# Two attention and expert layers on one core: loads reordered, first batch's layer norm in groups, clearing stores moved

## The chip, the cores and the metric

The kernel runs on one core of a Trainium2 chip. A core has five engines with their own instruction queues: TensorE (PE, matrix products), VectorE (DVE), ScalarE (ACT), GpSimd (POOL) and SyncE (SP, which here only issues transfers). Sixteen DMA engines move data between the chip's memory and the core's on-chip memory; SP, ACT and POOL can issue to them. The metric is the device time of one execution in microseconds (us). Before the change it is 3061.97 us, the median of 3 runs (3060.4 to 3063.5).

## The reference

Four sequences of 512 rows of 256 numbers (`x`) pass four layers, each added to `x`: a cross attention, a routed expert layer, a second cross attention, a second expert layer. The change touches the first alone:

```python
xn = _layernorm(x, gamma_media, beta_media)      # x here: the context, 4 x 1601 x 256
ln = _layernorm(latents, gamma_lat, beta_lat)    # latents: the normalised x, 4 x 512 x 256
q = ln @ Wq + bq
kv_input = jnp.concatenate([xn, ln], axis=1)
kv = kv_input @ Wkv + bkv
k, v = jnp.split(kv, 2, axis=-1)
...
sim = jnp.einsum('bhid,bhjd->bhij', q, k)        # 8 heads of 128
attn = jax.nn.softmax(sim, axis=-1)
out = jnp.einsum('bhij,bhjd->bhid', attn, v)
...
return out @ Wo + bo
```

The latents are normalised twice: once by the caller, once here with their own weights. Keys and values run over 512 + 1601 = 2113 positions. All numbers are float32.

## The kernel before

The kernel is written in a tile language: the source gives operations on tiles, and a scheduler decides the place of each operation in its engine's queue, from the dependences between tiles, from buffers coming free and from its own estimate of times. An engine works through its queue in that order, so an operation that waits holds up all that stand behind it on the same engine. The order in the source is a priority and no promise.

**Set-up (lines 66 to 332).** Constants and masks; among them `iota_i`, `lane_i` and `number_i` (lines 154, 306, 310), whole numbers that GpSimd writes and VectorE casts to float. `slot_x` and `rows_x` are tables in the chip's memory for the two expert layers. They are cleared once: `clear_slots` (line 147) with 8 stores of 512 KB issued by GpSimd, `clear_rows` (line 334) with 32 stores of 530 KB and one of 265 KB issued by SyncE, all out of a tile `empty`. `slot_x` is first written when batch 0 is routed, `rows_x` not before the last layer.

**First attention (lines 476 to 842).** Loads go out on SyncE in the order x of batch 0, seven small vectors (layer norm weights `gbm`, `gbl`, biases `bqk`), `bo`, the context of batch 0 as one transfer (12 tiles of 128 rows) and its tail of 65 rows, `wq`, `wkv`, `wo`, x of the other batches. `keys_input` (line 528) prepares a batch: `moments` (row statistics, bn_stats and bn_aggr, of 13 context tiles), `scale` (one square root on ScalarE for all tiles, then small VectorE operations, `ln_scale`, line 101), `latents` and `latents_again` (the two norms of x), `apply` (normalising the context, on VectorE), and `group` (line 551), which transposes four tiles on TensorE and evacuates them with the weights applied into `kvin`: channels 0 to 127 on VectorE, 128 to 255 on ScalarE. `kvin` holds position (k x 17 + c) x 32 + i at block c, quarter k, element i: each 128-wide block has 32 positions of each quarter of the sequence. The output bias `bo` gets the values' bias through `wo`: 8 rounds of a VectorE copy into `values_bias` and a product on TensorE (lines 742 to 749); `latents_again` adds `bo` to x on GpSimd.

`queries_keys(h)` (line 605) projects queries and keys of a head in six pieces, five of them keys, of 512 columns of `kvin` in the order of memory (the last of 128). `values` (line 648) projects the values for two heads in pieces of two blocks.

The loop at line 769 runs over n = batch x head x row tile, 128 steps. In step n: `scores` (5 products into the one buffer `ps_s`, then the maximum on VectorE, line 687), `turn` of the step before (a 32 x 32 transpose on VectorE, line 708), `softmax` (exponential on ScalarE, line 693), `exchange` (16 transfers of 68 KB between partition groups, 12 issued by SyncE and 4 by ScalarE, line 700), every second step `project`, and `weigh` (17 products for two row tiles, spread over two steps, line 716). `later[n]` holds pieces of other work for step n, such as the next head's keys. Before the loop, batch 0 is prepared in the order of the source (lines 751 to 756), then `empty` is set and both tables are cleared.

Transfers share eight completion semaphores for SyncE and ScalarE and eight for GpSimd. A transfer waits at issue until the one that holds its semaphore, in general the eighth before it, has landed.

Of the kernel before, what the change touches and what calls it, by code (L numbers as in the profile page):

```python
# [8 lines left out]
F32 = mybir.dt.float32  # L9
I32 = mybir.dt.int32  # L10
AF = mybir.ActivationFunctionType
ALU = mybir.AluOpType
# [4 lines left out]
P = 128  # L17
B, S, D = 4, 512, 256
M = 1601
NT = S // P  # L20
# [19 lines left out]
E, FF = 8, 1024  # L40
FC = FF // P
CAP = 2 * B * S // E
SLOTS = E * CAP
CT = CAP // P
NOWHERE = 65536.0
# [3 lines left out]
T = B * S  # L49
G = 256  # L50
GR = G // P
NG = (2 * T + E * (G - 1)) // G
ROWS = E * T
PAY = D + 1 + E
# [5 lines left out]
def rows_of(i, n, tail):  # L60
    return tail if i == n - 1 else P


@with_exitstack
def xattn_ffn_twice(ctx: ExitStack, tc: tile.TileContext, a: dict, out: bass.AP):
    nc = tc.nc

    const = ctx.enter_context(tc.tile_pool(name="const", bufs=1))
    dram = ctx.enter_context(tc.tile_pool(name="dram", bufs=1, space=DRAM))

    ident = const.tile([P, P], F32, name="ident")
    make_identity(nc, ident)

    flip = [0]

# [25 lines left out]
    def ln_scale(pool, mv, n):  # L101
        ve = pool.tile([P, n], F32, tag=f"ve{n}", name="ve")
        nc.vector.tensor_scalar(ve, mv[:, :, 1], EPS, None, ALU.add)
        rs = pool.tile([P, n], F32, tag=f"rs{n}", name="rs")
        nc.scalar.activation(rs, ve, AF.Sqrt)
        nc.vector.reciprocal(rs, rs)

        t = pool.tile([P, n], F32, tag=f"nt{n}", name="t")
        nc.vector.tensor_tensor(t, rs, rs, ALU.mult)
        nc.vector.tensor_tensor(t, t, ve, ALU.mult)  # L110
        nc.vector.tensor_scalar(t, t, -0.5, 1.5, ALU.mult, ALU.add)
        nc.vector.tensor_tensor(rs, rs, t, ALU.mult)
        return mv, rs
# [30 lines left out]
    slot_y = dram.tile([SLOTS, D], F32, name="slot_y")  # L144
    rows_x = dram.tile([ROWS + G, PAY], F32, name="rows_x")

    def clear_slots(zeros):
        for i in range(SLOTS // (4 * P)):
            nc.gpsimd.dma_start(
                slot_x[i * 4 * P : (i + 1) * 4 * P, :].rearrange("(p r) d -> p r d", p=P), zeros  # L150
            )


    iota_i = const.tile([P, NT, E], I32, name="iota_i")
    nc.gpsimd.iota(iota_i, pattern=[[0, NT], [1, E]], base=0, channel_multiplier=0)
    iota = const.tile([P, NT, E], F32, name="iota")
    nc.vector.tensor_copy(iota, iota_i)
# [4 lines left out]
    for r in (32, 96):  # L162
# [6 lines left out]
        fill=0.0,  # L169
# [133 lines left out]
                )  # L303


    lane_i = const.tile([P, 1], I32, name="lane_i")
    nc.gpsimd.iota(lane_i, pattern=[[0, 1]], base=0, channel_multiplier=1)
    lane = const.tile([P, 1], F32, name="lane")
    nc.vector.tensor_copy(lane, lane_i)
    number_i = const.tile([P, NG], I32, name="number_i")  # L310
    nc.gpsimd.iota(number_i, pattern=[[1, NG]], base=0, channel_multiplier=0)
    number = const.tile([P, NG], F32, name="number")
    nc.vector.tensor_copy(number, number_i)
    full = const.tile([P, T // G], F32, name="full")
    nc.vector.tensor_scalar(full, number[:, : T // G], float(G), None, ALU.mult)
    notafter = const.tile([P, E, E], F32, name="notafter")
# [14 lines left out]
        nc.sync.dma_start(rbias, a["br"].partition_broadcast(P))  # L331
        nc.sync.dma_start(b2, a["b2"])

    def clear_rows(empty):

        nc.gpsimd.memset(empty, 0.0)
        nc.gpsimd.memset(empty[:, :, D : D + 1], NOWHERE)
        n = ROWS // (4 * P)
        for i in range(n):
            nc.sync.dma_start(  # L340
                rows_x[i * 4 * P : (i + 1) * 4 * P, :].rearrange("(p r) d -> p r d", p=P), empty
            )
        nc.sync.dma_start(
            rows_x[ROWS:, :].rearrange("(p r) d -> p r d", p=P), empty[:, :GR, :]
        )

    def route2(b, two, psum, tag, first=0, n=NT):
# [128 lines left out]
    with ExitStack() as st:  # L476
# [10 lines left out]
        bqk = w.tile([P, 3, H0], F32, name="bqk")  # L487
        bo = w.tile([P, D], F32, name="bo")
        for dst, names in (
            (gbm, ("gamma_media", "beta_media")),  # L490
            (gbl, ("gamma_lat", "beta_lat")),
            (bqk, ("bq", "bk", "bv")),
        ):
            for k, name in enumerate(names):
                nc.sync.dma_start(dst[:, k, :], a[name])
        nc.sync.dma_start(bo, a["bo"].partition_broadcast(P))

        kvin = one.tile([P, DC, NB, 4, 32], F32, name="kvin")
        nc.vector.memset(kvin[:, :, NB - 2 :, 3, :], 0.0)
# [6 lines left out]
        def load_ctx(b):  # L506
            t = one.tile([P, NM, D], F32, tag="ctx", name="ctx_b")
            full = (NM - 1) * P
            nc.sync.dma_start(
                t[:, : NM - 1, :], a["ctx"][b, :full, :].rearrange("(t p) d -> p t d", p=P)  # L510
            )
            nc.sync.dma_start(t[:TAIL, NM - 1, :], a["ctx"][b, full:, :])
            return t

        ctx_b = load_ctx(0)

        wq = w.tile([P, DC, INNER], F32, name="wq")
        wkv = w.tile([P, DC, 2 * INNER], F32, name="wkv")
        wo = w.tile([P, H0, D], F32, name="wo")
        nc.sync.dma_start(wq, a["wq"].rearrange("(c p) f -> p c f", p=P))  # L520
        nc.sync.dma_start(wkv, a["wkv"].rearrange("(c p) f -> p c f", p=P))
        nc.sync.dma_start(wo, a["wo"].rearrange("(h p) d -> p h d", p=P))
        for b in range(1, B):
            load_x(b)
        nc.sync.dma_start(wr, a["w_router"].rearrange("(c p) e -> p c e", p=P))
        nc.sync.dma_start(bias, a["bias"].partition_broadcast(P))

        def keys_input(b, ctx_b):

# [11 lines left out]

            def latents_again():
                layernorm(two, state["lat"], state["lat"], NT)
                for i in range(NT):
                    nc.gpsimd.tensor_tensor(x[b][:, i, :], x[b][:, i, :], bo, ALU.add)

            def apply(n0):
                for i in range(n0, min(n0 + 4, NM)):
# [38 lines left out]
            def ctx_group(n0):  # L587
                group(ctx_b, n0, min(4, NM - n0), S + n0 * P, gbm, TAIL, NM)


            early = [
                lambda: moments(range(4)),
# [12 lines left out]
        def queries_keys(h):  # L605

            qT = two.tile([P, S], F32, tag="qT", name="qT")
            kT = two.tile([P, LP], F32, tag="kT", name="kT")
            hs = slice(h * DH0, (h + 1) * DH0)

            def queries():
                ps = ps_t.tile([P, 512], F32, tag="t", name="ps_q")
                for c in range(DC):
                    nc.tensor.matmul(
                        ps,
                        lhsT=wq[:, c, hs],
                        rhs=kvin[:, c, : S // 32, 0, :],
                        start=c == 0,
                        stop=c == DC - 1,
                    )  # L620
# [4 lines left out]
            def keys(j0):  # L625
                n = min(512, LP - j0)
                ps = ps_t.tile([P, 512], F32, tag="t", name="ps_k")
                for c in range(DC):
                    nc.tensor.matmul(  # L629
                        ps[:, :n],  # L630
                        lhsT=wkv[:, c, hs],
                        rhs=flat_kvin[c][:, j0 : j0 + n],
                        start=c == 0,
                        stop=c == DC - 1,
                    )
                nc.scalar.activation(  # L636
                    kT.rearrange("p (k b i) -> p b k i", k=4, i=32)[:, j0 // P : (j0 + n) // P],
                    ps[:, :n].rearrange("p (b k i) -> p b k i", k=4, i=32),
                    AF.Identity,
                    bias=bqk[:, 1, h : h + 1],  # L640
                )

            return qT, kT, [queries] + [lambda j0=j0: keys(j0) for j0 in range(0, LP, 512)]


        parts = (range(0, NB // 2 + 1), range(NB // 2 + 1, NB))
# [77 lines left out]
        def project(oT, inv, h, b, half):  # L724
# [9 lines left out]
            for k in range(2):  # L734
# [3 lines left out]
                    xs, ps[:, k, :], inv[:, t : t + 1], xs, ALU.mult, ALU.add  # L738
                )


        values_bias = w.tile([P, P], F32, name="values_bias")
        ps = ps_t.tile([P, D], F32, tag="t", name="ps_bo")
        for h in range(H0):
            nc.vector.tensor_copy(values_bias, bqk[:, 2, h : h + 1].to_broadcast([P, P]))
            nc.tensor.matmul(
                ps, lhsT=values_bias, rhs=wo[:, h, :], start=h == 0, stop=h == H0 - 1
            )
        nc.vector.tensor_tensor(bo, bo, ps, ALU.add)

        early, late = keys_input(0, ctx_b)
        for s in early + late:
            s()
        *qk, fill = queries_keys(0)
        for s in fill:
            s()
        empty = one.tile([P, 4, PAY], F32, tag="lat", name="empty")
        clear_rows(empty)
        clear_slots(empty[:, :, :D])
        load_second()  # L760


# [2 lines left out]
        later = [[] for _ in range(n_steps + 4)]  # L765
        tiles = {}
        v_of = [None, None]
        early = late = ()
        for n in range(n_steps + 4):
            b, h, t = n // (H0 * NT), n // NT % H0, n % NT  # L770
# [220 lines left out]
    with ExitStack() as st:  # L991
# [215 lines left out]
        at = {}  # L1207
# [94 lines left out]
    with ExitStack() as st:  # L1302
# [152 lines left out]
        ties = nc.values_load(n_over_i[0:1, 0:1], min_val=0, max_val=E * T)  # L1455
# [136 lines left out]
```

## Time and profile before

| | us |
|---|---|
| median of 3 runs | 3061.97 |
| the profiled execution, its own time | 3062.4 |
| its span, first to last instruction | 3060.7 |
| mean granted TensorE clock | 0.957 of full |
| start of the first exponential | 59.26 |
| clearing stores on GpSimd: start of the first, end of the last issue | 35.52, 44.99 |
| one issue of an exchange, median, SyncE and ScalarE (300 to 800 us) | 0.589, 0.605 |

A row of the timeline has the start and duration of a group of instructions in us, the engine, the line in the source, the operation, the tile written and the tiles read, the shape, the count, and in brackets how long the engine had idled and what ended that. A row of the stretches has the stretch, its length, then for PE, PEld (the loading of weights into TensorE, which overlaps), DVE, ACT and POOL the busy us and the number of instructions, then the granted clock, the mean busy share of the DMA engines and GB/s. A row of the DMA queues has packets, megabytes and the share of 16 engines' time; q0 is GpSimd's queue, q1 SyncE's, q10 ScalarE's.

### The profile page before, as it was taken

To read this page: it belongs to the slowest core of one execution; us is meant where nothing else is said; L and a number is where in the kernel's file an instruction comes from. 1 tells how busy PE (TensorE), PEld (TensorE's weight loads), DVE (VectorE), ACT (ScalarE), POOL (GpSimd) and SP (SyncE) were. 2 spreads that over 40 slices of the span, in tenths; PEclk is the share of its full clock that TensorE was granted. 3 is DMA by queue.
4 is the path that set the end of the run, shared out by engine and by line. 5 is a ranking of instruction groups with operands and counts; after the bars stand their busy time and mean duration, and the time that the engine had idled before them with its cause. 6 is when DMAs were issued, how large, how long until landed. Compare 5 with 4: busy or idle time off the path is not lost. (4 is left out here: it accounts for less than half of the span.)

```text
span 3060.7 us, 35871 instructions
## 1 busy us (share of the span) xinstructions
PE 2826.6 (92%) x13564; PEld 1885.8 (62%) x13564; DVE 1439.2 (47%) x2351; ACT 931.6 (30%) x1328; POOL 476.8 (16%) x347
## 2 busy tenths in 40 slices
PE   5899999999999999999997999599989897759999
PEld 2566666666666667676664666344545444448888
DVE  4365456544565444454443000577657566621111
ACT  2233234223342323323221211144334343412221
POOL 1000000100001000010001000333333333434442
PEclk9899999999999999999997999699999998969999
DMA  8543343343433433343333331300010100045562
GB/s 309 173 116 99 100 109 89 102 103 100 110 89 104 102 91 94 86 107 98 96 96 120 120 110 55 85 12 23 17 43 15 34 15 24 12 162 184 171 194 72
DMA packets 160942, 293.94 MB, mean 96 GB/s; under 512 B 42825, under 2 KB 78015, under 8 KB 157561
## 3 DMA queue, kind: packets, MB, share of 16 engines
q1 hardware_dynamic: 118280, 181.12, 21.3%
q0 software_dynamic: 17904, 74.77, 7.7%
q10 hardware_dynamic: 24576, 35.68, 4.5%
q8 instruction: 108, 1.77, 0.2%
q14 instruction: 74, 0.60, 0.1%
HBM read 100.24 MB, written 42.69 MB: 47 GB/s over the span
## 5 line engine op out<-in xcount | busy, mean ns | idle before, releaser
L687 DVE TENSOR_REDUCE top<-ps_s 128x1 f32<-128x2113 f32 x128 | 301.8, 2358 | 582.2 <-PE ps_s L679 576.6
L716 PE MATMUL ps_o<-pT,v 128*128 128x256 f32 x2176 | 521.6, 382 | 7.9 <-DVE pT L708 7.9
L679 PE MATMUL ps_s<-kT,qT 128*128 128x512 f32 (+1 forms) x1280 | 490.8, 528 | 15.2 <-ACT attn L693 14.7
L716 PEld LDWEIGHTS ps_o<-pT,v 128*128 128x128 f32 x2176 | 411.5, 192 | 125.1 <-issue 69.9
L679 PEld LDWEIGHTS ps_s<-kT,qT 128*128 128x128 f32 x1280 | 242.6, 191 | 265.7 <-issue 240.8
L693 ACT ACTIVATE attn<-ps_s,top 128x2113 f32<-128x2113 f32 x128 | 258.9, 2023 | 475.7 <-DVE top L687 411.2
L708 DVE STREAM_TRANSPOSE pT<-swapped 128x2176 f32<-128x2176 f32 x128 | 312.4, 2440 | 58.1 <-DMA swapped<-attn 48.2
L1080 DVE TENSOR_REDUCE tops<-ps_s 128x2 f32<-128x800 f32 (+1 forms) x256 | 243.0, 982 | 84.8 <-PE ps_s L1072 84.4
L1119 PE MATMUL ps_w<-asked,keyed 64*128 64x256 f32 (+1 forms) x1664 | 241.6, 422 | 41.0 <-DVE tops L1080 38.9
L629 PE MATMUL ps_k<-kvin,wkv 128*128 128x512 f32 (+1 forms) x640 | 262.1, 534 | 4.2 <-ACT kT L636 4.2
L1141 POOL TENSOR_TENSOR sum<-sum,pT 128x1024 f32<-128x1024 f32 x80 | 201.0, 2513 | 390.6 <-PE ps_o L1150 201.3
L662 PE MATMUL ps_v<-wkv,kvin 128*128 128x256 f32 x1088 | 253.5, 381 | 0.0
L1132 ACT ACTIVATE pT<-ps_w 128x1024 f32<-128x1024 f32 (+1 forms) x176 | 176.1, 1023 | 221.5 <-PE ps_w L1119 219.7
L1119 PEld LDWEIGHTS ps_w<-asked,keyed 64*128 64x128 f32 (+1 forms) x1664 | 156.0, 196 | 134.2 <-DVE tops L1080 74.4
L662 PEld LDWEIGHTS ps_v<-wkv,kvin 128*128 128x128 f32 x1088 | 204.9, 190 | 32.6 <-issue 3.3
L1072 PE MATMUL ps_s<-kT,qT 32*128 32x400 f32 (+1 forms) x1024 | 162.1, 588 | 30.1 <-DVE tops L1080 27.9
L1141 DVE TENSOR_TENSOR sum<-sum,pT 128x1024 f32<-128x1024 f32 x96 | 144.0, 1500 | 91.2 <-ACT pT L1132 78.0
L636 ACT ACTIVATE kT<-ps_k,bqk 128x512 f32<-128x512 f32 (+1 forms) x160 | 97.2, 620 | 268.2 <-PE ps_k L629 121.0
L629 PEld LDWEIGHTS ps_k<-kvin,wkv 128*128 128x128 f32 x640 | 116.5, 192 | 80.0 <-issue 67.1
L1417 PE MATMUL ps_h<-xT,w_e 128*128 128x256 f32 x736 | 164.7, 383 | 0.0
L1436 PE MATMUL ps_y<-w_e,hT 128*128 128x256 f32 x736 | 162.5, 379 | 0.0
L1417 PEld LDWEIGHTS ps_h<-xT,w_e 128*128 128x128 f32 x736 | 141.4, 192 | 19.6
(239 smaller groups left out, 2599.2 us busy)
## 6 DMA issues: line engine op xcount, KB each, us to landing
swapped<-attn SPq DMA_DIRECT2D x1536, 68.0 KB
swapped<-attn ACTq DMA_DIRECT2D x512, 68.0 KB
rows_x<-empty SPq DMA_DIRECT2D x32, 530.0 KB
w<-in_w_dram SPq DMA_DIRECT2D x16, 1024.0 KB
cT<-in_ctxT_dram SPq DMA_DIRECT2D x4, 1601.0 KB
keyed<-kT SPq DMA_DIRECT2D x32, 200.1 KB
ctx_b<-in_ctx_dram SPq DMA_DIRECT2D x4, 1536.0 KB
slot_x<-empty POOLq DMA_DIRECT2D x8, 512.0 KB
```

The source lines that it names most:

```text
L629: nc.tensor.matmul(ps[:, :n], lhsT=wkv[:, c, hs], rhs=flat_kvin[c][:, j0 : j0 + n], start=c == 0, stop=c == DC - 1,)
L662: nc.tensor.matmul(ps[:, k, :], lhsT=flat_kvin[c][:, j * P : (j + 1) * P], rhs=wkv[:, c, cols], start=c == 0, stop=c == DC - 1,)
L679: nc.tensor.matmul(flat[:, j0 : j0 + n], lhsT=qT[:, t * P : (t + 1) * P], rhs=kT[:, j0 : j0 + n], start=True, stop=True,)
L687: nc.vector.tensor_reduce(top, flat[:, :L], AX.X, ALU.max, negate=True)
L693: nc.scalar.activation(attn[:, :L], flat[:, :L], AF.Exp, bias=top, accum_out=total)
L708: nc.vector.transpose(pT[:, :, k * P : (k + 1) * P].rearrange("p c (a i) -> p a c i", a=4), swapped.rearrange("p a (c i) -> p a c i", i=32),)
L716: nc.tensor.matmul(ps, lhsT=v[:, j - parts[part][0], (h % 2) * DH0 : (h % 2 + 1) * DH0], rhs=pT[:, j, :], start=j == 0, stop=j == NB - 1,)
L1080: nc.vector.tensor_reduce(tops[u][:, t, 2 * pair : 2 * pair + 2, k], pss[pair][:, :, : hi - lo], AX.X, ALU.max,)
L1119: nc.tensor.matmul(ps[:r, s, pair * QH : (pair + 1) * QH], lhsT=keyed[o][64 * s : 64 * s + 64, pair, j * P : j * P + r], rhs=asked[u % 3][ ...
L1132: nc.scalar.activation(pT[:r], ps[:r], AF.Exp)
L1141: (nc.gpsimd if k else nc.vector).tensor_tensor(to, to, pT[:r], ALU.add)
L1417: nc.tensor.matmul(ps[:, f, :], lhsT=w[:, at : at + P], rhs=xT[:, c, :], start=c == 0, stop=c == DC - 1,)
```

## The change

Six things, all in the first attention and its set-up:

1. SyncE loads x of batch 0, then context tiles in fours, with the first head's columns of `wq` and `wkv` after the first four, then the tail, the values' half of `wkv`, and the rest. The seven small vectors go to ScalarE's queue.
2. Batch 0's context norm is done per group of four tiles: `first(n0)` takes statistics, scale, and applies the norm on ScalarE (an activation with scale and bias) instead of VectorE. Batches 1 to 3 keep the old steps.
3. `keys(k)` projects a quarter k (16 blocks, 512 columns with a stride) and, as fifth piece, the 17th block of all quarters.
4. The preparation of batch 0 is written out by hand and kept in that order on TensorE, VectorE, ScalarE and GpSimd: a wrapper round the engines marks the operations while `nc.kept[0]` is set. It begins with the latents; queries and the first key quarter follow before the second context group.
5. The clearing stores are put into `later` of steps 4 to 11 (`clear_slots`) and 16, 19, ... 112 (`clear_rows`), all on GpSimd, from a one-row `empty` read repeatedly. `empty` has a place of its own.
6. The output bias is computed in step 13, in the buffer of `lat`, with its addition to batch 0's x. The integer temporaries of the set-up live in a pool that is closed after them.

Since the wrapper makes the calls, a profile of the changed kernel gives one line, that of the wrapper (74), for most operations.

```diff
+class InOrder:
...
+        def call(*args, **kwargs):
+            ins = f(*args, **kwargs)
+            if self.kept[0]:
+                self.tc.keep_in_program_order(ins)
+            return ins
...
-    nc = tc.nc
+    nc = Engines(tc)
...
+    def clear_slots(zeros, i):
+        nc.gpsimd.dma_start(
+            slot_x[i * 4 * P : (i + 1) * 4 * P, :].rearrange("(p r) d -> p r d", p=P),
+            zeros.unsqueeze(1).to_broadcast([P, 4, D]),
+        )
+
+    brief_of = ExitStack()
+    brief = brief_of.enter_context(tc.tile_pool(name="brief", bufs=1))
...
-    number_i = const.tile([P, NG], I32, name="number_i")
+    number_i = brief.tile([P, NG], I32, name="number_i")
     nc.gpsimd.iota(number_i, pattern=[[1, NG]], base=0, channel_multiplier=0)
     number = const.tile([P, NG], F32, name="number")
     nc.vector.tensor_copy(number, number_i)
+    brief_of.close()
...
+    def clear_rows(empty, i):
+
+        at = slice(i * 4 * P, min((i + 1) * 4 * P, ROWS + G))
+        r = (at.stop - at.start) // P
+        nc.gpsimd.dma_start(
+            rows_x[at, :].rearrange("(p r) d -> p r d", p=P),
+            empty.unsqueeze(1).to_broadcast([P, r, PAY]),
         )
...
             for k, name in enumerate(names):
-                nc.sync.dma_start(dst[:, k, :], a[name])
-        nc.sync.dma_start(bo, a["bo"].partition_broadcast(P))
+                nc.scalar.dma_start(dst[:, k, :], a[name])
...
+        for n0 in range(0, NM - 1, 4):
+            nc.sync.dma_start(ctx_b[:, n0 : n0 + 4, :], of_ctx[:, n0 : n0 + 4, :])
+            if n0 == 0:
+                nc.sync.dma_start(wq[:, :, :DH0], of_wq[:, :, :DH0])
+                nc.sync.dma_start(wkv[:, :, :DH0], of_wkv[:, :, :DH0])
+        nc.sync.dma_start(ctx_b[:TAIL, NM - 1, :], a["ctx"][0, (NM - 1) * P :, :])
+        nc.sync.dma_start(wkv[:, :, INNER:], of_wkv[:, :, INNER:])
+        nc.sync.dma_start(wq[:, :, DH0:], of_wq[:, :, DH0:])
+        nc.sync.dma_start(wkv[:, :, DH0:INNER], of_wkv[:, :, DH0:INNER])
         nc.sync.dma_start(wo, a["wo"].rearrange("(h p) d -> p h d", p=P))
+        nc.sync.dma_start(bo, a["bo"].partition_broadcast(P))
...
+            def first(n0):
+
+                n = min(4, NM - n0)
+                mv = two.tile([P, 4, 2], F32, tag="mv4", name="mv_g")
...
+                    nc.vector.bn_stats(st[:r], ctx_b[:r, n0 + i, :])
+                    nc.vector.bn_aggr(mv[:r, i, :], st[:r])
+                mv, rs = ln_scale(two, mv, 4)
+                away = two.tile([P, 4], F32, tag="nt4", name="away")
+                nc.vector.scalar_tensor_tensor(away, mv[:, :, 0], -1.0, rs, ALU.mult, ALU.mult)
...
+                    nc.scalar.activation(
+                        of, of, AF.Identity, scale=rs[:r, i : i + 1], bias=away[:r, i : i + 1]
+                    )
...
+            def keys(k):
+
+                n = 512 if k < 4 else P
...
-                        rhs=flat_kvin[c][:, j0 : j0 + n],
+                        rhs=kvin[:, c, : NB - 1, k, :] if k < 4 else kvin[:, c, NB - 1, :, :],
...
+        def output_bias():
+
+            values_bias = one.tile([P, NT, D], F32, tag="lat", name="values_bias")[:, 0, :P]
...
+            nc.vector.tensor_tensor(bo, bo, ps, ALU.add)
+            add_output_bias(0)
+
+        nc.kept[0] = True
+        latent, context = keys_input(0, ctx_b)
+        *qk, fill = queries_keys(0)
+
+        stats, turns = context[::2], context[1::2]
+        for s in (
+            latent[:2] + stats[:1] + latent[2:] + fill[:2] + stats[1:2] + turns[:1] + stats[2:3]
+            + turns[1:2] + fill[2:3] + stats[3:] + turns[2:3] + fill[3:4] + turns[3:] + fill[4:]
+        ):
             s()
+        nc.kept[0] = False
+        empty = w.tile([P, PAY], F32, name="empty")
+        nc.gpsimd.memset(empty, 0.0)
+        nc.gpsimd.memset(empty[:, D : D + 1], NOWHERE)
         load_second()
...
+        for i in range(SLOTS // (4 * P)):
+            later[4 + i].append(lambda i=i: clear_slots(empty[:, :D], i))
+        for i in range(-(-(ROWS + G) // (4 * P))):
+            later[16 + 3 * i].append(lambda i=i: clear_rows(empty, i))
+        later[13].append(output_bias)
```

More of the change, by code (lines that the diff above doesn't have):

```diff
@@ L61, in rows_of, with __init__, __getattr__ @@
     return tail if i == n - 1 else P
+class InOrder:
+    def __init__(self, tc, engine, kept):
+        self.tc, self.engine, self.kept = tc, engine, kept
+    def __getattr__(self, name):
+        f = getattr(self.engine, name)
+        def call(*args, **kwargs):
[3 more added lines that the diff above has]
+            return ins
+        return call
+class Engines:
+    def __init__(self, tc):
+        self.kept = [False]
+        self.tensor, self.vector, self.scalar, self.gpsimd = (
+            InOrder(tc, e, self.kept) for e in (tc.nc.tensor, tc.nc.vector, tc.nc.scalar, tc.nc.gpsimd)
+        )
+        self.sync = tc.nc.sync
 @with_exitstack
 def xattn_ffn_twice(ctx: ExitStack, tc: tile.TileContext, a: dict, out: bass.AP):
-    nc = tc.nc
+    nc = Engines(tc)
     const = ctx.enter_context(tc.tile_pool(name="const", bufs=1))
@@ L71, in xattn_ffn_twice @@
     ident = const.tile([P, P], F32, name="ident")
-    make_identity(nc, ident)
+    make_identity(tc.nc, ident)
     flip = [0]
@@ L145, in xattn_ffn_twice @@
     rows_x = dram.tile([ROWS + G, PAY], F32, name="rows_x")
[L147 to L154, printed above, removed]
+    def clear_slots(zeros, i):
[5 more added lines that the diff above has]
+    brief = brief_of.enter_context(tc.tile_pool(name="brief", bufs=1))
+    iota_i = brief.tile([P, NT, E], I32, name="iota_i")
     nc.gpsimd.iota(iota_i, pattern=[[0, NT], [1, E]], base=0, channel_multiplier=0)
@@ L303, in add_collected @@
                 )
-    lane_i = const.tile([P, 1], I32, name="lane_i")
+    lane_i = brief.tile([P, 1], I32, name="lane_i")
     nc.gpsimd.iota(lane_i, pattern=[[0, 1]], base=0, channel_multiplier=1)
@@ L332, in load_second @@
         nc.sync.dma_start(b2, a["b2"])
[L334 to L344, printed above, removed]
+    def clear_rows(empty, i):
[4 more added lines that the diff above has]
+            empty.unsqueeze(1).to_broadcast([P, r, PAY]),
         )
@@ L489, in xattn_ffn_twice @@
         for dst, names in (
+            (gbl, ("gamma_lat", "beta_lat")),
             (gbm, ("gamma_media", "beta_media")),
-            (gbl, ("gamma_lat", "beta_lat")),
             (bqk, ("bq", "bk", "bv")),
@@ L513, in load_ctx @@
             return t
-        ctx_b = load_ctx(0)
         wq = w.tile([P, DC, INNER], F32, name="wq")
@@ L519, in xattn_ffn_twice @@
         wo = w.tile([P, H0, D], F32, name="wo")
-        nc.sync.dma_start(wq, a["wq"].rearrange("(c p) f -> p c f", p=P))
-        nc.sync.dma_start(wkv, a["wkv"].rearrange("(c p) f -> p c f", p=P))
+        of_wq = a["wq"].rearrange("(c p) f -> p c f", p=P)
+        of_wkv = a["wkv"].rearrange("(c p) f -> p c f", p=P)
+        ctx_b = one.tile([P, NM, D], F32, tag="ctx", name="ctx_b")
+        of_ctx = a["ctx"][0, : (NM - 1) * P, :].rearrange("(t p) d -> p t d", p=P)
+        for n0 in range(0, NM - 1, 4):
[7 more added lines that the diff above has]
+        nc.sync.dma_start(wkv[:, :, DH0:INNER], of_wkv[:, :, DH0:INNER])
         nc.sync.dma_start(wo, a["wo"].rearrange("(h p) d -> p h d", p=P))
+        nc.sync.dma_start(bo, a["bo"].partition_broadcast(P))
         for b in range(1, B):
@@ L526, in xattn_ffn_twice, with add_output_bias @@
         nc.sync.dma_start(bias, a["bias"].partition_broadcast(P))
+        def add_output_bias(b):
+            for i in range(NT):
+                nc.gpsimd.tensor_tensor(x[b][:, i, :], x[b][:, i, :], bo, ALU.add)
         def keys_input(b, ctx_b):
@@ L543, in latents_again @@
                 layernorm(two, state["lat"], state["lat"], NT)
-                for i in range(NT):
-                    nc.gpsimd.tensor_tensor(x[b][:, i, :], x[b][:, i, :], bo, ALU.add)
+                if b:
+                    add_output_bias(b)
             def apply(n0):
@@ L588, in ctx_group @@
                 group(ctx_b, n0, min(4, NM - n0), S + n0 * P, gbm, TAIL, NM)
+            def first(n0):
+                n = min(4, NM - n0)
+                mv = two.tile([P, 4, 2], F32, tag="mv4", name="mv_g")
+                if n < 4:
+                    nc.vector.memset(mv, 1.0)
+                for i in range(n):
+                    r = rows_of(n0 + i, NM, TAIL)
+                    st = two.tile([P, 6], F32, tag="bnst", name="st")
+                    nc.vector.bn_stats(st[:r], ctx_b[:r, n0 + i, :])
[3 more added lines that the diff above has]
+                nc.vector.scalar_tensor_tensor(away, mv[:, :, 0], -1.0, rs, ALU.mult, ALU.mult)
+                for i in range(n):
+                    r = rows_of(n0 + i, NM, TAIL)
+                    of = ctx_b[:r, n0 + i, :]
+                    nc.scalar.activation(
+                        of, of, AF.Identity, scale=rs[:r, i : i + 1], bias=away[:r, i : i + 1]
+                    )
+            if b == 0:
+                steps = [latents, latents_again, lambda: group(state["lat"], 0, NT, 0, gbl, P, NT)]
+                return steps, [
+                    f for n0 in range(0, NM, 4) for f in (lambda n0=n0: first(n0), lambda n0=n0: ctx_group(n0))
+                ]
             early = [
@@ L623, in queries @@
                 )
-            def keys(j0):
-                n = min(512, LP - j0)
+            def keys(k):
+                n = 512 if k < 4 else P
                 ps = ps_t.tile([P, 512], F32, tag="t", name="ps_k")
@@ L635, in keys @@
                     )
[L636 to L643, printed above, removed]
+                to = kT.rearrange("p (k j) -> p k j", k=4)
+                of = ps[:, :n]
+                if k < 4:
+                    to = to[:, k, : W4 - 32]
+                else:
+                    to, of = to[:, :, W4 - 32 :], of.rearrange("p (k i) -> p k i", k=4)
+                nc.scalar.activation(to, of, AF.Identity, bias=bqk[:, 1, h : h + 1])
+            return qT, kT, [queries] + [lambda k=k: keys(k) for k in range(5)]
         parts = (range(0, NB // 2 + 1), range(NB // 2 + 1, NB))
@@ L739, in project @@
                 )
[L742 to L752, printed above, removed]
-            s()
[L754 to L759, printed above, removed]
+        def output_bias():
+            values_bias = one.tile([P, NT, D], F32, tag="lat", name="values_bias")[:, 0, :P]
+            ps = ps_t.tile([P, D], F32, tag="t", name="ps_bo")
+            for h in range(H0):
+                nc.vector.tensor_copy(values_bias, bqk[:, 2, h : h + 1].to_broadcast([P, P]))
+                nc.tensor.matmul(
+                    ps, lhsT=values_bias, rhs=wo[:, h, :], start=h == 0, stop=h == H0 - 1
+                )
+            nc.vector.tensor_tensor(bo, bo, ps, ALU.add)
[8 more added lines that the diff above has]
+        ):
+            s()
+        nc.kept[0] = False
+        empty = w.tile([P, PAY], F32, name="empty")
+        nc.gpsimd.memset(empty, 0.0)
+        nc.gpsimd.memset(empty[:, D : D + 1], NOWHERE)
         load_second()
@@ L1454, in xattn_ffn_twice @@
         nc.vector.tensor_copy(n_over_i, n_over)
-        ties = nc.values_load(n_over_i[0:1, 0:1], min_val=0, max_val=E * T)
+        ties = tc.nc.values_load(n_over_i[0:1, 0:1], min_val=0, max_val=E * T)
         spare = st.enter_context(tc.tile_pool(name="d_spare", bufs=1))
```

## The prediction

> **What bounds the kernel now.** I read the engine shares first, then the busy time in stretches of the first 200 us, then the timelines of TensorE, VectorE and SyncE there. The shares:
>
> ```profile
> span 3060.7 us, 35871 instructions
> PE 2826.6 (92%) x13564; PEld 1885.8 (62%) x13564; DVE 1439.2 (47%) x2351; ACT 931.6 (30%) x1328; POOL 476.8 (16%) x347
> ```
>
> TensorE is the bound, so a change pays where TensorE idles. The stretches say where that is, before 160 us (the clock follows the four busy times):
>
> ```profile
> 0.00:40.00 40.00, 10.74 (x40) 6.35 (x40) 23.55 (x124) 3.71 (x7) 6.67 (x22) 1.00 0.67 239
> 40.00:80.00 40.00, 34.14 (x89) 16.07 (x88) 8.46 (x11) 13.98 (x21) 4.98 (x7) 0.91 1.02 387
> 80.00:120.00 40.00, 28.36 (x94) 19.11 (x93) 10.25 (x7) 9.96 (x14) 0.00 (x0) 0.81 0.66 213
> 120.00:160.00 40.00, 38.91 (x141) 26.05 (x141) 21.27 (x15) 10.64 (x13) 0.00 (x0) 0.98 0.42 105
> 160.00:200.00 40.00, 40.00 (x148) 27.09 (x147) 20.92 (x23) 12.15 (x19) 0.00 (x0) 1.00 0.54 144
> ```
>
> Idle: 29.3 + 5.9 + 11.6 + 1.1 = 47.9 us; from 160 us on the attention has none. The whole change lies there. TensorE's timeline gives its marks:
>
> ```profile
> 43.36 1.96 PE L614 MATMUL ps_q<-kvin,wq 128*128 128x512 f32 x4
> 52.95 3.87 PE L679 MATMUL ps_s<-kT,qT 128*128 128x512 f32 x10 [0.33 <-ACT kT L636]
> 105.69 6.68 PE L679 MATMUL ps_s<-kT,qT 128*128 128x512 f32 x10 [7.05 <-ACT attn L693]
> 118.84 5.43 PE L716 MATMUL ps_o<-pT,v 128*128 128x256 f32 x18
> ```
>
> Queries begin at 43.4, first scores at 53, first weighing of values at 118.8: I use the last as finish line. By then four full scores, all 17 value blocks and part of head 2's projections are done. Two delays lead there. The first is VectorE, which starts on the context at 13.4; the second is the first exchange:
>
> ```profile
> 13.38 0.75 DVE L93 BATCH_NORM_STATS2 st<-ctx_b 128x6 f32<-128x256 f32 x2 [6.60 <-DMA ctx_b<-in_ctx_dram]
> 103.48 2.44 DVE L708 STREAM_TRANSPOSE pT<-swapped 128x2176 f32<-128x2176 f32 x1 [20.68 <-DMA swapped<-attn]
> ```
>
> The first softmax starts at 59.26; its transposed probabilities come 44 us later. SyncE's own timeline shows why:
>
> ```profile
> 35.62 52.70 SPq L340 DMA_DIRECT2D rows_x<-empty  x32
> 88.36 1.28 SPq L343 DMA_DIRECT2D rows_x<-empty  x1
> ```
>
> SyncE issues 33 clearing stores until 89.6; the exchanges stand behind them.
>
> **The Trainium skill.** "DMA: Bandwidth & Descriptors", section "Issuing engines are not separate DMA queues": all queues run on the same 16 engines, another issuer saves only issue time. The 40-80 row agrees: DMA share 1.02 with two queues filled. Same page, "Queues, rings and completion order": each engine alternates between its queues, packet by packet. From 47 to 60 us the trace has
>
> ```profile
> q1 hardware_dynamic: 668, 2.53, 51.0%
> q0 software_dynamic: 665, 2.43, 50.4%
> ```
>
> equal packets and bytes, with 4 KB packets on both sides; what 1 KB rows get beside 4 KB ones no row shows. "TensorE: Matmul & The Clock Gate", Part 1: after about 3.4 us of idleness the clock halves. Here it was 0.54 from 70 to 75 us after a 4.18 us wait, and ten score matmuls took 6.68 instead of 3.77 us.
>
> **The change, part by part.** Order and waits I read from the two built programs.
>
> (a) The clearing stores do not come where the loop writes them. They need only `empty`, so the scheduler sets all 41 at the head of GpSimd's queue. `empty` waits for VectorE's cast of `number_i`, behind the first four statistics. x0 is about 0.5 MB, moved at 248 GB/s between 2 and 4 us, so statistics start near 4.5; four pairs take 2.1, a small operation 0.2, the casts 0.5: 7.4 us. The stores' data flow from about 10 us, at most eight in flight, against the loads. SyncE is freed: exchanges wait no more behind 33 issues, but share the engines. 21.5 MB of stores, 5 MB of loads still due and 1.6 MB of batch 1's context at 0.39 MB/us last until about 82 us.
>
> (b) Latents first. `gbl` sits where the casts' temporaries were, so its load, first of seven on ScalarE's queue, also waits for 7.4 us. Four issues took 2.44 us, 0.61 each; bq's waits for x1 to land (2.7 MB at 0.39 from 2.1 us: about 10), the last ends near 11.8. Behind them stand the table load (1.28) and the first square root (0.2). So the latents go on at S = 14, no earlier than the context does now. Bounds: 10.5 if the issues overlap, 19 if x1 is late.
>
> (c) The ordered chain after S, from rows now. Latents twice: 1.0 for five small operations, 1.4 for four applications, 2.1 statistics, 0.5 for the root, 1.0 and 1.4 again: 7.4. Group 0 statistics and scale 3.8, plus 1.0 for a copy (`values_bias`) that waits for the latents' transposes: 12.2. ScalarE applies (4 x 0.39), evacuates (0.78), queries 1.0, qT 0.75: 16.3. Group 1: 3.8, evacuation 1.0, group 2: 3.8, evacuation 1.0: 25.9. From here VectorE, ScalarE and TensorE hand over in turn: group 2's application and group 1's evacuation 1.6, key matmul 1.0, kT 0.7, root and scale of the last tile 1.4, apply 0.4, evacuation 1.0, matmul 1.0, transposes 0.5, evacuation 0.9, two key pieces 1.4, kT 0.8, four score pieces 3.0, maximum 2.4: S + 42. Bursts with gaps over 3.4 us (before key quarter 1) cost about 3 at the half clock: first exponential at 59, as now (59.26). The context's application moves to ScalarE at no cost, since ScalarE is 30% busy.
>
> (d) Batch 1's context load and norm move to the first steps: nothing holds them back. The load starts when the last transpose frees the buffer, about 51. At equal shares 1.6 MB take 8.4, and landing about 2 (the load of bv: issue over at 4.65, its first reader at 6.12): L = 61.5. On VectorE 16 pairs (7.7 us for 17 now) stand in front of the second maximum, and on ScalarE an exchange issue waits for the load too. So: second maximum 69.2 to 71.6, exponential to 73.8, 13 applications and scale 5.1 to 76.7, first transpose 79.1 (the exchange, 12 issues of 0.59 on SyncE and 2 to land, 9 us, came meanwhile), third maximum 81.5, exponential 83.7, fourth scores and three value pieces 6.4: 90.1. To the finish line: 16 value products of 0.44, queries and keys 3.8, one score piece 0.8, 11.6: 101.7, that is L + 40. Gain 118.8 - 101.7 = 17.1.
>
> (e) The output bias moves from idle time into step 13. Sixteen 256-wide matmuls at 0.22 are 3.5. Each pair waits for a VectorE copy, one of these behind a transpose; TensorE's order puts keys, scores and weighing between, which hides the 1 us round trips. Bounds 3.5 and 8; I take 3.5.
>
> (f) Keys by quarter: strided reads cost nothing, since queries have them now (592 ns median, as keys). No step in the rest gains an instruction.
>
> Sum: -17.1 + 3.5 = -13.6; -13, since the hand-overs carry no tenths. The profiled execution took 3062.4 (span 3060.7), 0.4 above the median 3061.97: 3049.
>
> **Rivals.** One formula serves: change = L + 40.2 + 3.5 - 118.8 = L - 75.
> 1. The context load starves (against: the equal shares above; for: its rows are 1 KB, and at one packet each it gets 46 of 211 ns). 96 rows per engine then take 20 us, L = 72: -3, no change that counts. 3059.
> 2. The start works as named: S = 10.5, no half clock, L = 54: -21, less 3 of slow clock now lost at 70-120: 3038.
> 3. Slower: the stores take the engines until they are through. L = 85, exchange 0 issues only then, and the chain of (d) runs from there: +10, 3072. It decides from L = 75, and is measurable from 81.
> 4. It does not do what it says: stores are not dealt out. That is in (a), not apart.
>
> **How the numbers follow.** Forecast (3040 to 3056 by itself) 0.45, rival 2 0.13, rival 1 0.24, rival 3 0.18. A measurement tells 0.2%, 6 us, from none. Faster: forecast, rival 2 and a little of rival 1, 0.59; same 0.23; slower 0.18. Range from rival 2 with (e) at its low end and some luck to rival 3: 3032 to 3071.
>
> **What would show it.** GpSimd's clearing stores from about 8 us; seven loads then a table load on ScalarE until 13; first exponential near 59; batch 1's statistics on VectorE near 61; first transposition near 77; first weighing near 102; TensorE idle before 160 us cut from 48 to about 35. A first exponential far below 55, or context statistics after 75, proves the working wrong.

## The result, and the profile after

The changed kernel takes 3116.64 us (median of 4 runs, 3115.07 to 3118.38) beside 3061.18 us for the kernel before on the same chip: a ratio of 1.0174, 95% interval 1.0160 to 1.0188. It is slower by 55 us, where the prediction said 13 us faster. The profiled execution took 3115.07 us, its span is 3113.3 us, 52.6 us more than the span before.

The shares of the page:

```profile
span 3113.3 us, 35886 instructions
PE 2833.9 (91%) x13564; PEld 1888.6 (61%) x13564; DVE 1439.3 (46%) x2360; ACT 941.7 (30%) x1346; POOL 499.9 (16%) x380
```

TensorE is busy for 7.3 us more (2833.9 against 2826.6); the other 45 us are idleness. The stretches of the first 200 us, in the same columns as before, say where:

```profile
0.00:40.00 40.00, 10.88 (x30) 5.15 (x30) 21.37 (x106) 8.37 (x17) 15.90 (x35) 0.99 0.99 331
40.00:80.00 40.00, 25.72 (x64) 11.50 (x64) 8.40 (x26) 11.86 (x22) 10.28 (x15) 0.80 1.06 242
80.00:120.00 40.00, 1.45 (x2) 0.84 (x3) 3.74 (x18) 1.97 (x2) 5.66 (x8) 0.50 0.97 238
120.00:160.00 40.00, 35.17 (x124) 23.47 (x122) 24.14 (x53) 16.93 (x23) 0.00 (x0) 0.86 0.39 95
160.00:200.00 40.00, 40.00 (x142) 25.60 (x142) 21.66 (x17) 11.88 (x15) 0.00 (x0) 1.00 0.40 98
```

From 80 to 120 us TensorE works 1.45 us, and the other engines do little too; only the DMA engines are full (share 0.97). Yet they move 238 GB/s, where two full queues moved 387 before the change. The row for 160 to 200 is full again, as before.

What they all wait for is batch 1's context. The rows of the timelines of VectorE, TensorE and ScalarE that end the gap:

```profile
116.26 0.75 DVE L74 BATCH_NORM_STATS2 st<-ctx_b 128x6 f32<-128x256 f32 x2 [52.60 <-DMA ctx_b<-in_ctx_dram]
118.55 3.78 PE L74 MATMUL ps_k<-kvin,wkv 128*128 128x512 f32 x4 [47.49 <-ACT kT L74]
76.36 41.41 ACTq L74 DMA_DIRECT2D swapped<-attn  x4
117.81 0.69 ACT L74 ACTIVATE kT<-ps_k,bqk 128x512 f32<-128x512 f32 x1 [52.10 <-DMA ctx_b<-in_ctx_dram]
```

VectorE had idled 52.6 us for it. ScalarE stood in its four exchange issues for 41.4 us, with the key evacuation behind them, and TensorE behind that. So L, the landing that the prediction put at 61.5, is 116.3.

The issues on SyncE and GpSimd:

```profile
58.78 3.39 SPq L536 DMA_DIRECT2D ctx_b<-in_ctx_dram  x1
62.22 28.35 SPq L539 DMA_DIRECT2D ctx_b<-in_ctx_dram  x1
90.66 31.91 SPq L771 DMA_DIRECT2D swapped<-attn  x12
```

```profile
7.53 0.49 POOL L74 MEMSET empty<- 128x265 f32 x2 [5.02 <-DVE number L74]
7.95 6.26 POOL L74 DMA_DIRECT2D slot_x<-empty  x8
13.69 1.27 POOL L74 DMA_DIRECT2D rows_x<-empty  x1
```

The clearing stores leave from 8 us, as predicted, and the last is issued at 99. The context's load is issued at 58.8, its tail stands at issue until 90.6, and the exchanges behind it.

How the loads fared beside the stores shows best from 70 to 85 us, in the view of the DMA queues (packets, MB, share of the 16 engines' time):

```profile
DMA packets 1675, 3.33 MB, mean 222 GB/s; under 512 B 746, under 2 KB 922, under 8 KB 1675
q0 software_dynamic: 813, 3.06, 91.8%
q1 hardware_dynamic: 814, 0.20, 11.9%
```

The two queues got 813 and 814 packets: the same number, though GpSimd's carried 3.06 MB and SyncE's 0.20. In this stretch SyncE's queue is delivering the routers' weights and the second router's bias, rows of 32 bytes. The packet records give the sizes: between 68 and 85 us there are 640 packets of 32 bytes, 20 KB in all, with some 200 rows of 1 KB and the transfers' semaphore writes among them. A row of 32 bytes waits for its turn behind a store's packet of 4240 bytes much as a row of 1 KB does: SyncE's queue gets 54 packets per us here (814 in 15 us), and 53 from 90 to 110 us (1052 in 20 us), where all its rows have 1 KB.

The lag of a kernel behind the one before, in us, read at the starts of the exponentials (the exponential of step n has number n), separates the losses in time. Negative is ahead:

| exponential | before, us | after | dealt | e2 | e2r2late | bkeys |
|---|---|---|---|---|---|---|
| 0 | 59.26 | +3.8 | +1.7 | -6.6 | -5.0 | -0.1 |
| 1 | 72.00 | +53.6 | -1.0 | -5.0 | -5.0 | +0.5 |
| 2 | 103.53 | +33.5 | -22.0 | -25.1 | -28.1 | -0.7 |
| 7 | 158.58 | +35.2 | -20.4 | -23.4 | -26.0 | -1.3 |
| 14 | 244.55 | +39.1 | -16.5 | -22.7 | -25.9 | -1.1 |
| 71 | 931.95 | +38.9 | -16.4 | -22.2 | -26.4 | -1.4 |
| 74 | 966.09 | +46.1 | -6.2 | -12.0 | -22.4 | -1.4 |
| 127 | 1600.21 | +46.0 | -6.4 | -11.4 | -19.4 | -1.6 |

After: +35.2 from the start, +3.9 at step 13, +7 at step 72, and 6.6 between the end of the attention and the end of the program. The other columns are experiments.

The loss at step 72 is a second stall, which no step of the prediction had. TensorE's timeline:

```profile
978.98 0.41 PE L74 MATMUL ps_c<-cnt,before 128*128 128x32 f32 x2 [2.29 <-DVE cnt L74]
981.48 1.22 PE L74 MATMUL ps_k<-kvin,wkv 128*128 128x128 f32 x4 [0.87 <-DVE x L74]
991.91 1.12 PE L74 MATMUL ps_s<-kT,qT 128*128 128x512 f32 x2 [1.97 <-ACT attn L74]
```

`ps_c` counts the rows that batch 1's routing sends to each expert. In the changed kernel the scheduler has put it, for this batch alone, behind 17 of that step's value products instead of 10, with the next step's key, query and score products behind it. TensorE waits there for VectorE's count (2.3 us), and twice more until 992 (0.9 us for VectorE, 2.0 us for ScalarE).

### The profile page after: what moved, and what is told of

It reads as the page before. It is cut to its first block, busy times and chain, and to the rows that moved or that the text cites. A ratio compares the mean times of both kernels' runs of the same rounds, so it can differ in the third digit from the quotient of the medians.

```text
span 3113.3 us, 35886 instructions
## 1 busy us (share of the span) xinstructions
PE 2833.9 (91%) x13564; PEld 1888.6 (61%) x13564; DVE 1439.3 (46%) x2360; ACT 941.7 (30%) x1346; POOL 499.9 (16%) x380
## 5 line engine op out<-in xcount | busy, mean ns | idle before, releaser
L74 PE MATMUL ps_s<-kT,qT 128*128 128x512 f32 (+3 forms) x2304 | 652.9, 553 | 42.4 <-DVE tops L74 32.7
L74 PE MATMUL ps_o<-pT,v 128*128 128x256 f32 (+2 forms) x3584 | 624.4, 388 | 7.6 <-DVE pT L74 7.6
L74 PEld LDWEIGHTS ps_o<-pT,v 128*128 128x128 f32 (+2 forms) x3584 | 446.9, 160 | 162.6 <-issue 94.1
L74 PEld LDWEIGHTS ps_s<-kT,qT 128*128 128x128 f32 (+1 forms) x2304 | 298.6, 194 | 369.2 <-issue 276.5
L74 ACT COPY v<-ps_v 128x512 f32<-128x512 f32 (+1 forms) x165 | 91.6, 560 | 266.5 <-PE ps_v L74 196.2
```

The source lines that it names most:

```text
L74: ins = f(*args, **kwargs)
```

## The experiments

Twelve more kernels ran. Theory A is the one that the view of the queues suggests: the DMA engines give each queue a turn per packet, so SyncE's loads advance by rows and not by bytes while the stores run. Its rivals are theory B, that the stores' bytes hold the engines until they are through (batch 1's context landed just when the stores ended, at 116), and theory C, that the new load order delays the context by itself.

**dealt: the stores really dealt out.** Ahead of each store a column of `empty` is written again from a result of the step that the source names:

```diff
+        def held(store, what, i):
+            nc.gpsimd.tensor_scalar(empty[:, :1], now[0], 0.0, None, ALU.mult)
+            store(what, i)
...
-            later[4 + i].append(lambda i=i: clear_slots(empty[:, :D], i))
+            later[4 + i].append(lambda i=i: held(clear_slots, empty[:, :D], i))
...
+                now[0] = inv[:, t : t + 1]
```

> The changed kernel with the clearing stores really dealt out: ahead of each store one column of the empty tile is written again from a result of the step it was meant for, so no store can leave before that step. Theory A (the stores' early start starves the loads): batch 1's context lands near 61 us, as the prediction had it, the second exponential starts below 76 us, and the time is 3117 - (116 - 61) = about 3062, or 3049 if the later losses of 13 us go too. Theory C (the new order of the loads and SyncE's waits for semaphores delay the context by themselves): it lands after 90 us and the time stays above 3090.

Measured: 3056.19 us, ratio 0.9984 (0.9977 to 0.9991), 60 us less than the changed kernel. VectorE's timeline:

```profile
58.56 2.36 DVE L74 TENSOR_REDUCE top<-ps_s 128x1 f32<-128x2113 f32 x1 [6.95 <-PE ps_s L74]
61.49 0.74 DVE L74 BATCH_NORM_STATS2 st<-ctx_b 128x6 f32<-128x256 f32 x2
68.45 2.33 DVE L74 TENSOR_REDUCE top<-ps_s 128x1 f32<-128x2113 f32 x1
76.76 2.44 DVE L74 STREAM_TRANSPOSE pT<-swapped 128x2176 f32<-128x2176 f32 x1 [0.26 <-DMA swapped<-attn]
```

The statistics start at 61.5 without a wait, the second maximum at 68.5, the first transposition at 76.8. The whole context went through between 51 and 61 us, with SyncE's queue alone; by the packet records its 1601 rows took from 53.1 to 58.4 us:

```profile
DMA packets 1630, 1.64 MB, mean 164 GB/s; under 512 B 29, under 2 KB 1630, under 8 KB 1630
q1 hardware_dynamic: 1630, 1.64, 51.4%
```

The load order is the same here, so theory C falls: the early stores cost the 55 us of the start (+35.2 against -20.4 at exponential 7). The losses at steps 13 and 72 stay (3.8 and 10 us), which is why even this kernel is only 6 us faster than the one before.

**rgp: 640 tiny rows on the other queue.** The two routers' weights and the second router's bias are issued by GpSimd, ahead of its stores (`nc.sync.dma_start` becomes `nc.gpsimd.dma_start` for `wr`, `wr2` and `rbias`).

> The changed kernel with three tiny loads (the two routers' weights and the second router's bias, 640 rows of 32 bytes, 20 KB in all) issued by GpSimd ahead of its stores instead of by SyncE ahead of batch 1's context. Theory A (a turn per packet): SyncE's queue has 640 packets less ahead of the context; at 54 packets per us that is 12 us, so the context lands at about 104 us instead of 116 and the time falls to about 3105. Theory B (bytes decide): 20 KB are 0.1 us at 0.2 MB per us; it lands at 116 and the time stays at 3117.

Measured: 3095.87 us, ratio 1.0100 (1.0079 to 1.0120). VectorE's timeline, and the queues from 100 to 108 us:

```profile
98.88 0.75 DVE L74 BATCH_NORM_STATS2 st<-ctx_b 128x6 f32<-128x256 f32 x2 [33.20 <-DMA ctx_b<-in_ctx_dram]
```

```profile
q0 software_dynamic: 485, 1.82, 89.1%
q1 hardware_dynamic: 135, 0.20, 9.1%
```

20 KB moved to the other queue bring the context forward by 17 us, where bytes would have given 0.1; and the stores still fill 89% of the engines after it has landed. Theory B falls. The 5 us more than the expected 12 come mostly from the rate, by the packet records: from 24 us to the landing SyncE's queue passed 58 packets per us instead of 55, most of all from 24 to 40 us (68 instead of 60), where the stores, now behind the tiny loads, ran 2 us later. The load is also issued earlier (54.6 instead of 58.8), but rows of earlier loads were still in the queue then, so that by itself explains nothing.

**small: the stores row by row.** Both tables are cleared in the order `(r p) d` instead of `(p r) d`, meant to make GpSimd's packets a quarter as large.

> The changed kernel with one edit: each clearing store writes its rows as single rows of 1060 (1024) bytes instead of four rows together, so that GpSimd's packets have a quarter of the size at the same bytes. Theory A (the two queues alternate packet for packet, so a load's packet of 1 KB waits for a store's packet of 4 KB, whatever its own size): SyncE's queue gets about 150 packets per us instead of 54, batch 1's context lands at about 70 us instead of 116, and the time falls by about 45 us to about 3071. Theory B (the stores' bytes hold the engines until they are through, whatever the size of packets): it lands at 116 or later, and the time stays at 3117 or above.

Measured: 3096.84 us, ratio 1.0117 (1.0097 to 1.0136), the context at 99.4. The edit did not do what it was for: the packets still had 4240 bytes, four rows of 1060. It does not test the size, but shows two other things. The counts stay equal (from 58 to 95 us 2522 packets on GpSimd's queue, 2523 on SyncE's), and a packet of 4240 bytes took 212 ns on average instead of 271, so that both queues went through 68 packets per us instead of 54. The landing follows that rate: from 24 us on about 5000 packets were due in both kernels (92 us at 54, 75 at 68).

**bstores: the stores moved alone.** In the kernel before, only the 33 stores of `clear_rows` go from SyncE to GpSimd.

> The kernel before with one edit: the 33 stores that clear the rows are issued by GpSimd instead of SyncE; they still start at 35 us, when nearly all loads have landed. Theory A: only the context of batch 1 (1601 rows of 1 KB) is left beside them; at 54 packets per us it lands near 66 us, SyncE's exchanges no longer stand behind 33 issues, and the time falls by about 10 us to 3050. Theory B (GpSimd's stores hold the engines until through, to about 110 us): the context lands after 100 us and the time rises by 20 us or more.

Measured: 3076.09 us, ratio 1.0043 (1.0028 to 1.0058): slower by 14, where theory A had been taken to give 12 faster. VectorE's timeline:

```profile
69.56 0.75 DVE L93 BATCH_NORM_STATS2 st<-ctx_b 128x6 f32<-128x256 f32 x2 [23.52 <-DMA ctx_b<-in_ctx_dram]
77.01 2.34 DVE L687 TENSOR_REDUCE top<-ps_s 128x1 f32<-128x2113 f32 x1
```

The landing is as theory A has it (69.6, expected 66; theory B said over 100), at 82 packets per us from 58 to 68. The step from it to the time was wrong: here batch 1's statistics stand ahead of the first maximum, not of the second. VectorE waits 23.5 us, the first exponential comes 20 us later, and the lag stays at +8.3. The same load is harmful or not by what the scheduler puts behind it.

**clate: the context held back, the stores early.** In the changed kernel a column of the context's buffer is written from a result of step 15 before the load.

```diff
+            if b == 1:
+                for i in (0, NM - 1):
+                    nc.vector.tensor_scalar(t[:, i, :1], now[0], 0.0, None, ALU.mult)
```

> The changed kernel with its early stores, but batch 1's context is not loaded before step 16: a column of its buffer is written first from a result of step 15. So its statistics no longer stand in front of the second maximum. Theory D (the stores hurt only through this one load): the first exchange goes out near 65 us, the first transposition comes near 76, and the time is about 3052. Theory A (every transfer of SyncE and ScalarE takes turns with the stores, and their semaphores wait for the loads queued ahead, so the exchanges starve as well): first transposition near 100 us, time about 3078.

Measured: 3081.75 us, ratio 1.0063 (1.0046 to 1.0080). The first exchange is issued at 64.6, and yet (ScalarE and VectorE):

```profile
64.61 21.46 ACTq L74 DMA_DIRECT2D swapped<-attn  x4
101.94 2.44 DVE L74 STREAM_TRANSPOSE pT<-swapped 128x2176 f32<-128x2176 f32 x1 [12.36 <-DMA swapped<-attn]
```

Its four issues on ScalarE take 21 us, and the transposition waits until 102 (expected 100 by A, 76 by D). The time is near theory A's 3078 as well, so theory D falls: the context was the worst of several transfers that starve, not the only one.

**bias0 and dealt0: the bias in step 0.** `later[13].append(output_bias)` becomes `later[0].append(output_bias)`, in the changed kernel and in the one with the stores dealt out.

> The changed kernel with the output bias computed in step 0, where TensorE idles, instead of step 13. If the product of step 13 costs what its busy time shows (4.8 us): about 3112. If the loss at that place came from something else: 3117.

> The kernel with the stores really dealt out (run before), with the output bias computed in step 0 instead of step 13. In step 0 TensorE still waits for other work, in step 13 it doesn't: the 4 us of lag that come up at step 13 go, and about 3052 follows. If the VectorE copies between the eight products now stand in front of batch 1's statistics: no gain, 3056.

Measured: bias0 3106.63 us (ratio 1.0145, 1.0125 to 1.0166), dealt0 3057.14 us (0.9981, 0.9973 to 0.9988). In both the lag at step 13 is gone, so it was this product. In bias0 another 6 us go, by accident: the addition to x stands in GpSimd's queue ahead of the last eight stores and waits until 108.7. From 87 to 95 us, while the stores run dry, SyncE's queue has 803 packets and GpSimd's 306, and the context lands at 99.6. In dealt0 nothing is gained, as its second alternative said: on VectorE the copies and batch 1's statistics take turns, exponential 1 starts at 74.9 us instead of 71.0, and the lag at exponential 7 is -15.5 instead of -20.4.

**bkeys: the keys alone.** The kernel before with `keys`, and the evacuation that belongs to it, of the changed one.

> The kernel before with one edit, the keys projected by quarter of the sequence. The prediction put it at nothing: 3062, same. If strided columns cost TensorE or ScalarE time in each of 128 steps: 3066 or more.

Measured: 3060.79 us, ratio 0.9997 (0.9987 to 1.0007).

**e2, e2r2, e2late, e2r2late: what a better version needs.** All have the stores dealt out and the bias in step 0. In e2 `nc.sync` loads the seven vectors, and the tile of `bo` is laid out ahead of theirs; in e2r2 the routing starts at `t == 2` instead of `t == 1`; "late" holds batch 1's context back as in clate.

> As the run with the bias in step 0, and the seven small vectors go to SyncE behind x and the context, so that ScalarE can load its table at once. If ScalarE's seven issues set the start of the latents (15.4 us after the change): the first square root comes at about 9, the first exponential at about 55 instead of 61, batch 1's context lands near 55, and the time is about 3046. If the loads of the first head's weights set the pace instead: first exponential at 60 or later, 3052.

> As the run before in this list, and the routing of a batch starts one step later. The lag of 7 to 10 us that comes up at exponential 72 in each form of the changed kernel is put down to the scheduler's place for batch 1's routing counts, ahead of which TensorE waits for VectorE. If that is so, the lag of batch 1 goes and the time is about 3038; if the other place is as bad, or it was something else, 3046 or more.

> As the run with the stores really dealt out, the bias in step 0 and the seven vectors on SyncE (e2), with batch 1's context held back to step 16 as well. In e2 the second maximum waits until VectorE is through with batch 1's statistics, and the third exponential starts at 78 us. If that wait is the next bound: third exponential near 68, time 3048 - 10 = about 3038. If the exchange comes no earlier: 3048.

> As the run before in this list, and the routing starts one step later (e2r2). That took the lag at exponential 72 away once, but lost 3 to 5 us at other steps; about 3036 if the two edits add, 3040 or more if not.

| | us | ratio to before | 95% |
|---|---|---|---|
| e2 | 3048.47 | 0.9953 | 0.9936 to 0.9969 |
| e2r2 | 3049.88 | 0.9955 | 0.9939 to 0.9970 |
| e2late | 3047.41 | 0.9953 | 0.9937 to 0.9970 |
| e2r2late | 3042.17 | 0.9933 | 0.9916 to 0.9950 |

In e2 ScalarE's timeline has the table load at the head, and the first root waits for its input alone:

```profile
0.79 1.28 ACT L74 ACT_TABLE_LOAD   x1 [0.79 <-PEq L1669]
7.27 0.20 ACT L74 ACTIVATE rs<-ve 128x4 f32<-128x4 f32 x1 [5.20 <-DVE ve L74]
```

The start of that root, which stands for the prediction's S, falls from 13.8 (dealt0) to 7.3 us, and the first exponential comes 7.9 us earlier than in dealt0: the seven issues ahead of the table load were on the path. In e2r2 the lag at exponential 72 does not come up (-23.5 at 71, -23.6 at 72), so the place of the routing is its cause; but 4 us are lost at the very next step and 3 later, so that e2r2 misses its 3038, and the medians of e2 and e2r2 don't differ. e2late misses its number too: the third exponential comes at 75.3, not 68. By TensorE's timeline the bias product is now in the way: the last six of its eight pairs, each after a copy on VectorE, come one every 1.3 us between keys and the second scores. With both edits the time is 3042.17 us (3036 was expected if they add): 0.7% below the kernel before, the best version found, faster than both kernels.

## Why the prediction was wrong

**(a) Half right.** The stores left from 8 us and were not dealt out, as said. "At equal shares" was taken in bytes, and that is wrong: the shares are equal in packets. The Trainium skill's page "DMA: Bandwidth & Descriptors", section "Queues, rings and completion order", has the turn per packet, and the prediction cited it; its check was a stretch where both queues had 4 KB packets, so that packets and bytes could not be told apart. The page's typical packet of 9 to 17 descriptors did not show here: the packets held four rows on GpSimd's queue and one row on SyncE's. Nor did 0.39 MB per us hold: from 40 to 120 us it was 0.24, and the stores lasted to about 116 us instead of 82.

**(b), (c) Nearly right.** S, the latents' first square root, was 15.2 (predicted 14), the first exponential 63.0 (59). The context's applications took 0.5 us each instead of 0.39, and the queries and two key quarters took 3.4 to 3.8 us each instead of 1.9, where the prediction had one key quarter. The granted clock was 0.55 and 0.53 in the two key quarters (its records begin at 32.3 us, after the queries). No wait of TensorE in the 6 us before either of them was longer than 1.7 us, so the gaps of 3.4 us that the prediction looked for are not the measure here; several short ones were enough here. Its own figures for the clock come from two places: 0.54 after the wait of 4.18 us, but the 6.68 us of ten score products after one of 7.05.

**(d) The step that failed:** "At equal shares 1.6 MB take 8.4, and landing about 2 (...): L = 61.5." L was 116.3. The load was issued at 58.8 instead of 51: the buffer came free at 54, and until 58 SyncE's earlier issues waited for starved loads. Some 500 rows of x, 128 rows of `bias` and 640 rows of 32 bytes were still ahead in SyncE's queue then, until about 84. Its own 1601 rows followed at 54 packets per us, 30 us. The prediction priced one load on an empty queue. Rival 1 did the same with the right turn, 211 ns for a packet of each queue (and 96 of the 100 rows per engine), and so came to 72 only. (Rival 2's L of 54 is 55 by its own terms.) What had to be counted is every row still in the queue; it was in the order of the loads, which the prediction knew. What follows L was right: with the stores held back (dealt) the statistics started at 61.5, the second maximum came at 68.5 (69.2), the first transposition at 76.8 (76.7 to 79.1), TensorE idled 35.2 us before 160 us (35). That the 61.5 agrees to the tenth is luck: the context's last row was through at 58.4, with no stores beside it, and VectorE was busy until 61.5 with the first maximum and the queries. And with the measured L of the changed kernel the formula L - 75 gives +41 for the change, where the lag at exponential 14 is +39.1.

**(e) Right in size:** 3.9 us of lag, 4.8 us of busy time, without waits, as the group of TensorE's products has it:

```profile
L74 PE MATMUL ps_bo<-wo,values_bias 128*128 128x256 f32 x16 | 4.8, 379 | 0.0
```

**(f) Right:** the keys by quarter change nothing (0.9997).

**What it did not have.** The 7 us at step 72 (10 in dealt, with step 73) are 900 us away from the last line that the change touches. The prediction had said "No step in the rest gains an instruction", which is true, and took it for no loss. The order of TensorE's instructions in both built programs, which it drew on for the start alone, would have shown it. What in the change moves the scheduler there is open; neither the keys nor the stores alone do (bkeys and bstores have no such lag). Of the 6.6 us after the attention the cause is open too: in the other runs that stretch took between 2 us less (e2r2) and 11 us more (bstores) than before, with no pattern that follows the edits.

**The sum.** Predicted -13.6; L adds 54.8, which makes +41.2; measured at exponential 14 is +39.1, then 7 at step 72 and 6.6 after: 52.7, the difference of the two profiled times (3115.07 - 3062.4). Rival 3 had the sign, by another mechanism, with L = 85. What spoke for rival 1 (its rows are 1 KB, the stores' packets 4 KB) was the stronger evidence, and it was set aside for a stretch that could not tell.

## What to carry to other kernels

Beside a bulk transfer of large packets on another queue, price a load by the packets still ahead of it in its queue, and not by its bytes: here 640 rows of 32 bytes cost about as much as 640 rows of 1 KB. Work without a dependence is not "dealt out" by where a loop writes it; tie it to a result of the step in which it is to leave. After a change to a scheduled kernel compare the order of instructions over the whole program, also far from the edit.

## What was not expected of the hardware

Packets of the same 4240 bytes took different times, on average over all 4160 of them by the packet records: 172 ns with four rows lying side by side in the source and the target (bstores), 212 with one source row read again and single target rows (small), 271 with one source row read four times for four neighbouring target rows (after). Beside the slow ones the loads' own 1 KB packets took about 75 ns instead of 46. So part of the delay comes from longer turns, and not from the number of turns.

The form of the store alone does not explain it. In the changed kernel the first eight stores, those of `slot_x`, have the same form with rows of 1024 bytes instead of 1060, and their packets of 4096 bytes took 162 ns. In dealt the stores of `rows_x` have the slow form, but are spread over the attention, and took 204 ns. Why they are slower beside the loads is open; a full `empty` in the changed kernel was not tried.
